# Attention with a top-1 expert layer on one core: a re-planned agenda of projections, with the bias moved to VectorE

## The chip, the core and the metric

One NeuronCore of a Trainium2 chip runs the whole kernel in one launch. The metric is the device time in microseconds. All data is fp32 unless a line says otherwise.

## The reference

`x` has the shape 4 x 2048 x 512. A layer norm without gain gives `xn`. Two branches read `xn`, and both are added to `x`:

```python
qkv = xn @ w_qkv                               # 16 heads of 32
q, k = spectral_filter(q, mask), spectral_filter(k, mask)
attn = softmax(q @ k.T / sqrt(32)) @ v
attention = attn @ w_out + b_out

probs = softmax(xn @ w_gate)                   # 8 experts, top 1, 100 slots each
expert = gate * (xn_of_slot @ w_expert + b_expert)   # first 100 tokens of each expert
out = x + attention + expert
```

The filter is a fixed 32 x 32 map on each head, so the kernel folds it once into the query and key columns of `w_qkv`.

## The kernel before

**Units of work.** Work is cut by batch (4) and by group of four heads (4 per batch): 16 groups, numbered `k`. For a group the kernel walks over four blocks of 512 queries, and in a block over 16 tiles of 128 keys. One key tile against 512 queries for four heads is called a *half* here (two of them make a `window` of the main loop). A block has 16 halves, a group 64, and the kernel 1024.

**What every half holds.** In order of emission, for the two pairs of heads: `max_matmuls` (two matmuls whose products only serve the row maxima, 40 items ahead of their use), `scores` (two matmuls into the four PSUM banks kept for scores), the exponential of those two heads on ScalarE, and `max_reduce` on VectorE. Then `products` (probabilities times values, of the half before) with `num += ...` on VectorE. Then whatever the agenda has for this half.

**Banks.** The other four PSUM banks go round in turn (`turns`, `bank()`): two for each `max_matmuls`, one for `products`, one for each further piece. A half with one piece takes six banks, one without takes five. `max_reduce` either reads both banks in one instruction, where they lie side by side (`joined`), or each by itself (`apart=True`), which lets the first go earlier.

**The agenda.** Before the main loop, `plan(k)` writes for every half which further pieces it emits. TensorE's pieces all cost about the same:

- `query_key` and `value`: 48 pieces a group, the projections of the next group (`projections(k + 1)` gives their order). `spread` places them by the costs already booked in each half, up to a half called `last`.
- `result`: 16 a group, a quarter of a block's output projection; `fold`: four a group, the sums of the probabilities. Both follow from the end of a block (`close_steps`): `fold` in its fifth half after, eight reciprocals (`invert`) in halves 6 to 13, results in halves 17 to 20.
- `turn`: 16 transposes of normalized rows in the last group of a batch.

Once per block the maxima are negated and transposed on TensorE (`max_close`, in the block's twelfth half), split into three bf16 parts on GpSimd (`max_split`) and sent by a small DMA (`negm<-row`); the next block begins with a matmul on them (`shift`).

**Around it.** GpSimd adds pairs of probability tiles (`even<-even`) after an accumulating DMA of its own queue (`even<-odd`) has added the odd tile to the even one. In the third group of a batch (k = 2, 6, 10) the next batch's rows are loaded on SP's queue, measured on VectorE (`measure`: `bn_stats`, `bn_aggr`), given the output bias on GpSimd (`bias`), and written to the output (`first_sums`); `scale` makes their factors on GpSimd. The first batch's rows get bias and first sums in group 0. Later every block's result is added to the output by an accumulating DMA from `y`.

All of these go through a helper that keeps each engine's program order, so nearly every instruction carries its line, 84. Tiles tell them apart.

Of the kernel before, what the change touches and what calls it, by code (L numbers as in the profile page):

```python
# [103 lines left out]
def attention_and_top1_experts(ctx: ExitStack, tc: tile.TileContext, a: dict, out: bass.AP):  # L104
# [90 lines left out]
    def filter_steps(c):  # L195

        held = {}

        def turned(s):
            if s == 0:  # L200
                held["wt"] = probs(c % 2 == 1)
            pt = bank()
            for r in range(NR):
                on.tensor.transpose(
                    pt[:, r * P : (r + 1) * P], raw[s, r // 2][:, r % 2, c * P : (c + 1) * P], ident
                )
            on.vector.tensor_copy(held["wt"][:, s, 0, :], pt)

        def filtered(s):
            pw = bank()  # L210
            wt = held["wt"][:, s]
            for r in range(NR):
                at = slice(r * P, (r + 1) * P)
                on.tensor.matmul(pw[:, at], lhsT=wt[:, 0, at], rhs=filt, start=True, stop=True)
            done = pw.rearrange("p (r n) -> p r n", r=NR)
            if c == 0:
                on.scalar.copy(wg[0][:, :, s, :], done)
# [12 lines left out]
    def token_stage(b):  # L230
# [19 lines left out]

        def bias(i):
            row = held[i // TQ][:, i % TQ, :]
            on.gpsimd.tensor_tensor(row, row, b_out, ALU.add)

        def first_sums(i):

            n, t = divmod(i, TQ)
            on.sync.dma_start(out=o[b, n, :, t : t + 1, :], in_=held[n][:, t : t + 1, :])

# [147 lines left out]
        route += [lambda i=i: enter(i) for i in range(NT)]  # L407
        return load, measure, scale, normalize, turn, route, bias, first_sums, load_tile

# [3 lines left out]

    def load_qkv_weights(k):
        wg[k] = weights.tile([P, NR, 3, P], F32, name="wg", bufs=1)
        on.sync.dma_start(out=wg[k], in_=wd[k % NG])

# [11 lines left out]
    def query_key(k, n, s, first, last):  # L429
# [3 lines left out]
        for r in range(NR):  # L433
            columns(pq, wg[k][:, r, s, :], xnT[:, r, cols], start=(r == 0), stop=(r == NR - 1))
        if s == 0:
# [16 lines left out]
    def value(k, n, first, last):  # L452
# [3 lines left out]
        for t in range(first, last):  # L456
            i = n * TQ + t
            for r in range(NR):
                columns(
                    pv[:, t * P : (t + 1) * P],  # L460
                    xnT[:, r, i * P : (i + 1) * P],
                    wg[k][:, r, 2, :],
                    start=(r == 0),
# [4 lines left out]

    def projections(k, tiles=1):

# [4 lines left out]
        else:  # L475
            late = [(value, n) for n in range(2, NQ)] + [(query_key, 1, 0)]
            order = [(query_key, 0, 0)] + [(value, n) for n in range(2)] + (late if k not in CROWDED else [])
            order += [(query_key, n, 1) for n in range(NQ)] + (late[::-1] if k in CROWDED else [])
            order += [(query_key, n, 0) for n in range(2, NQ)]
        return [  # L480
# [71 lines left out]
    def expert_steps():  # L552


        def begin():
            w_exp = chunk("w_exp")
            on.sync.dma_start(out=w_exp, in_=a["L0_ffn_w_expert"].rearrange("(r p) n -> p r n", p=P))
            b_exp = b_out
            on.sync.dma_start(out=b_exp, in_=a["L0_ffn_b_expert"].partition_broadcast(P))
# [129 lines left out]
    def close_steps(k, n):  # L689
# [49 lines left out]

    load, measure, scale, normalize, turn, first_route, first_bias, first_sums, load_tile = token_stage(0)  # L740

# [3 lines left out]
    load(3, probs(False).rearrange("p u h q -> p (u h) q"))  # L745
    wg[0] = weights.tile([P, NR, 3, P], F32, name="wg", bufs=1)
    nc.sync.dma_start(out=wg[0][:, :, 2, :], in_=w_qkv[:, :, 2 * DM : 2 * DM + P])
    for c in range(1, NG):
# [4 lines left out]
    for i in range(2 * NG + 1):  # L753
# [4 lines left out]
        if 2 * NG - TQ <= i < 2 * NG:  # L758
            measure(i - 2 * NG + TQ)
    nc.sync.dma_start(out=wd[0], in_=wg[0])  # L760
    first_projections = projections(0, TQ)
# [50 lines left out]
    for i, item in enumerate(stream[:MAX_AHEAD]):  # L812
# [5 lines left out]
        max_matmuls(item, half)  # L818
        max_reduce(item, half)
        if i in ahead:  # L820
# [81 lines left out]

    def keys_from(k):

        return (9 if k in CROWDED else 6) * TQ

    def plan(k):
# [3 lines left out]

        def after_keys_are_spent(steps, start):

            first = len(steps) - keys_from(k + 1)
            for i in range(NT):
                cost, _, step = steps[first + i]
                steps[first + i] = cost, start + SPENT + i // TQ * TQ, step

        if k == 0:
            for i in range(NT):  # L920
                half = 2 + i + 5 * (i // TQ)
                at(half, load_tile, i)
                at(half + 4, first_bias, i)
                at(half + 6, first_sums, i)
# [4 lines left out]
        steps = []  # L929
        if k == 0:  # L930
            done = spread([(1, 0, step) for step in first_projections], 15)
            at(done[-1] + 1, load_qkv_weights, 1)
            plan_route(20, lambda i: first_route[i]())
            ready = done[-1] + 3
        if c == NG - 2 and b + 1 < B:

            at(start + 20, begin_stage, b + 1)
            for i in range(NT):
                half = start + 20 + i + 5 * (i // TQ)
                at(half, in_stage, 8, i)  # L940
                at(half + 3, in_stage, 1, i)
                at(half + 4, in_stage, 6, i)
                at(half + 6, in_stage, 7, i)
            for n in range(NQ):
                at(start + 30 + (TQ + 5) * n, in_stage, 2, n * TQ, (n + 1) * TQ)
            for i in range(2 * TQ):
                at(start + GH - 6 + i, in_stage, 8, i)
        pieces = projections(k + 1)
        if c == NG - 1:

            late = {8: 9, 12: 14}
            order = [("turn", i) for i in range(8)] + pieces[:4] + [("turn", i) for i in range(8, 12)]
            order += pieces[4:8] + [("turn", i) for i in range(12, NT)] + pieces[8:]
            steps, first = [], start + 1
# [6 lines left out]
            steps[0] = (1, first, steps[0][2])  # L961
            after_keys_are_spent(steps, start)
            done = spread(steps, last)
# [3 lines left out]
            for i in range(2 * TQ, NT):  # L967
                at(turned[i // TQ * TQ - TQ - 1] + 1 + i % TQ, in_stage, 8, i)
            plan_route(turned[NT - 1] + 2, follow_route)
        else:  # L970
            steps = [(1, ready if k == 0 else start, step) for step in pieces]
            after_keys_are_spent(steps, start)
            done = spread(steps, last)
        assert done[-4] >= start + 3 * HB and done[-8] >= start + 2 * HB
        for i in range(NT):
            here = done[len(done) - keys_from(k + 1) + i] - start - i // TQ * TQ
            assert SPENT <= here < SPENT + 3 * TQ
# [35 lines left out]
    for k in range(B * NG):  # L1013
        for n in range(NQ):
            num = work.tile([P, QB], F32, tag="num", name="num")
            tiles = {}
            for w in range(NW):
# [9 lines left out]
                for j in (even, odd):  # L1027
# [5 lines left out]
                    for u in range(2):  # L1033
# [72 lines left out]
```

## Time and profile before

| what | value |
|---|---|
| time, median of 3 runs | 4277.05 us (4273.49 to 4280.85) |
| the profiled execution | 4282.12 us, of which the span 4280.0 us |
| TensorE busy | 4194.3 us (98%) |
| VectorE, ScalarE, GpSimd busy | 3411.0 (80%), 2525.3 (59%), 3037.6 (71%) |
| reductions of maxima, 128x512 apart / 128x1024 joined | 2576 of 683 ns / 760 of 1217 ns |
| GpSimd's bias, 128x512 | 64 of 1546 ns |
| ScalarE's copy of a result | 252 of 586 ns |
| VectorE's add of a PSUM bank, 128x512 (`num`) | 960 of 677 ns |

Matmuls overlap each other in the array, and a matmul that is slow to end counts as busy, so the 98% does not say that TensorE is at its peak. A half's length is better read in the timeline, from the first weight load of its `keys,q` matmuls to that of the next half.

### The profile page before, as it was taken

Reading aid. Unit: us, or ns where it says so; the run is one execution under the profiler, and the core shown is the slowest. Engines: PE = TensorE matmul, PEld = TensorE weight load, DVE = VectorE, ACT = ScalarE, POOL = GpSimd, SP = SyncE. Lnnn points to the kernel's source line nnn. Section 1 sums busy time; section 2 is a strip of 40 time slices with the busy share of each in tenths; the row PEclk is TensorE's granted clock in tenths of the full one; section 3 lists DMA queues with packets and bytes.
Section 4 is the critical chain, followed back from the end, with each engine's and each line's share of the span. In section 5 each row is a group of like instructions: output and inputs, shape, how many; then the busy total and the mean of one; then the engine's idle time right before and its main releaser. Section 6 shows DMA issues by size and latency. Waiting matters only on the chain.

```text
span 4280.0 us, 120579 instructions
## 1 busy us (share of the span) xinstructions
PE 4194.3 (98%) x52270; PEld 1854.3 (43%) x52270; DVE 3411.0 (80%) x5102; ACT 2525.3 (59%) x3475; POOL 3037.6 (71%) x2110
## 2 busy tenths in 40 slices
PE   8999999999999999999999999999999999999998
PEld 4444444434444444443444444443444444444432
DVE  6767888877788888887778888887778887788885
ACT  2556655666566556557556666555755565556665
POOL 1678777876776767777677766778668776676773
PEclk9999999999999999999999999999999999999999
DMA  4767778887687778888677787888877886778788
GB/s 109 179 149 152 153 160 173 191 201 151 137 159 153 156 152 165 182 195 186 132 158 151 158 159 146 170 188 194 170 140 152 175 164 131 148 162 161 154 168 167
DMA packets 163452, 690.16 MB, mean 161 GB/s; under 512 B 27414, under 2 KB 32696, under 8 KB 97640
## 3 DMA queue, kind: packets, MB, share of 16 engines
q0 software_dynamic: 110432, 605.83, 72.1%
q1 hardware_dynamic: 51312, 76.10, 5.7%
q8 instruction: 409, 6.70, 0.6%
q14 instruction: 123, 1.01, 0.1%
q10 hardware_dynamic: 1176, 0.52, 0.1%
HBM read 59.27 MB, written 88.96 MB: 35 GB/s over the span
## 4 chain that ended last, share of the span: by engine, by line
PE 89%; DVE 6%; DMA 2%; POOL 2%; issue 1%; ACT 0%; ACTq 0%; POOLq 0%; DVEq 0%
PE array L84 89%; DVE part L84 4%; DMA even<-odd 2%; POOL even L84 1%; DVE num L84 0%; DVE stats L84 0%; DMA negm<-row 0%; DVE factor L84 0%; POOL xs L84 0%; DMA odd<-in_L_attn_w_qkv_dram 0%; DVE mv L84 0%; POOL row L84 0%; POOL rstd L84 0%; DVE even L84 0%; POOL rest L84 0%
## 5 line engine op out<-in xcount | busy, mean ns | idle before, releaser
L84 DVE TENSOR_REDUCE part<-array 128x1 f32<-128x512 f32 (+1 forms) x3336 | 2497.1, 805 | 761.6 <-PE array L84 758.3
L84 POOL TENSOR_TENSOR even<-even 128x1024 f32<-128x1024 f32 x876 | 2121.5, 2524 | 425.9 <-DMA even<-odd 417.8
L84 PE MATMUL array<-keys,q 32*128 32x512 f32 x8192 | 2089.7, 615 | 10.9 <-DVE part L84 5.5
L84 PE MATMUL array<-q,steps_of_keys 32*128 32x512 f32 x8192 | 2022.7, 618 | 3.3 <-ACT odd L84 1.7
L84 ACT ACTIVATE even<-array 128x1024 f32<-128x1024 f32 x1024 | 993.5, 1021 | 491.3 <-PE array L84 455.6
L84 ACT ACTIVATE odd<-array 128x1024 f32<-128x1024 f32 x1024 | 993.3, 1021 | 458.8 <-PE array L84 378.5
L84 PEld LDWEIGHTS array<-keys,q 32*128 32x128 f32 x8192 | 784.3, 185 | 591.3 <-DVE part L84 365.3
L84 PEld LDWEIGHTS array<-q,steps_of_keys 32*128 32x128 f32 x8192 | 707.2, 184 | 267.3 <-issue 233.1
L84 POOL DMA_DIRECT2D even<-odd x510 | 463.4, 909 | 402.2 <-ACT odd L84 321.4
L84 DVE TENSOR_TENSOR num<-num,array 128x512 f32<-128x512 f32 x960 | 650.3, 677 | 26.3 <-PE array L84 17.2
L84 PE MATMUL array<-odd,v 128*32 128x512 f32 x4096 | 549.4, 608 | 2.4 <-DVE part L84 2.4
L84 PE MATMUL array<-even,v 128*32 128x512 f32 x4096 | 547.4, 606 | 2.9 <-DVE part L84 2.9
L84 PEld LDWEIGHTS array<-xnT,wg 128*32 128x32 f32 x15808 | 439.0, 110 | 256.2 <-DVE part L84 176.2
L84 PE MATMUL array<-xnT,wg 128*32 128x128 f32 (+1 forms) x15808 | 522.0, 277 | 11.4 <-DVE part L84 10.6
L84 PEld LDWEIGHTS array<-wg,xnT 128*32 128x32 f32 x8192 | 227.9, 110 | 129.2 <-DVE part L84 94.4
L84 DVE RECIPROCAL factor<-den 128x64 f32<-128x64 f32 x504 | 274.3, 545 | 0.0
L84 PE MATMUL array<-wo,ot 128*32 128x512 f32 x2048 | 267.8, 596 | 4.0 <-POOL ot L84 4.0
L84 PE MATMUL array<-wg,xnT 128*32 128x128 f32 x8192 | 263.5, 273 | 4.4 <-DVE part L84 4.4
L84 PEld LDWEIGHTS array<-odd,v 128*32 128x32 f32 x4096 | 81.0, 108 | 394.1 <-DVE part L84 384.9
L84 PEld LDWEIGHTS array<-even,v 128*32 128x32 f32 x4096 | 80.8, 108 | 393.8 <-DVE part L84 382.7
L84 POOL DMA_DIRECT2D out_dram<-y x63 | 83.7, 1329 | 212.4 <-ACT y L84 190.9
L84 ACT COPY y<-array 128x512 f32<-128x512 f32 x252 | 147.5, 586 | 139.8 <-PE array L84 139.4
(129 smaller groups left out, 1490.5 us busy)
## 6 DMA issues: line engine op xcount, KB each, us to landing
even<-odd POOLq DMA_DIRECT2D x510, 1024.0 KB, 8.2
out_dram<-y POOLq DMA_DIRECT2D x63, 1024.0 KB, 10.1
xs<-in_L_attn_x_dram SPq DMA_DIRECT2D x112, 256.0 KB
out_dram<-xs SPq DMA_DIRECT2D x64, 256.0 KB
wg<-wd SPq DMA_DIRECT2D x15, 768.0 KB
wo<-in_L_attn_w_out_dram SPq DMA_DIRECT2D x16, 256.0 KB
negm<-row SPq DMA_DIRECT2D x192, 4.0 KB
xs<-in_L_attn_x_dram SPq DMA_DIRECT2D x2, 1024.0 KB
```

What stands on the lines that cost most here:

```text
L84: done = act(*args, **kwargs)
```

## The change

- `load_qkv_weights`: the next group's weights lie in three tiles (query, key, value), each loaded by itself when its own last piece is done.
- `projections`: most groups begin with all value pieces, then half of the queries, the keys, and the rest of the queries. `last` is the group's last half and no longer the fourth from its end; the extra cost booked in the half of `max_close` is 0.25 and no longer 0.5; a `turn` is booked at 0.5 and no longer at 1.
- `max_close` comes behind the half's agenda, not ahead of it.
- `bias` on GpSimd is gone: where k is a multiple of 4 (the first head group of a batch) `result` adds `b_out` on VectorE and the ScalarE copy is not made. `first_sums` is one DMA of 1 MB from the input to the output for each 512 rows, not four of 256 KB from SBUF. In group 0 the rows are not loaded again for it.
- In groups 2, 6 and 10 `measure` moves from halves 23 to 53 to halves 30 to 37 and 46 to 53, where no reciprocals are planned.
- `max_reduce` reads apart in every half for which nothing was booked; ahead of the main loop it reads joined wherever it can.
- The experts' bias has a tile of its own.

```diff
 def load_qkv_weights(k, s):
-    wg[k] = weights.tile([P, NR, 3, P], F32, name="wg", bufs=1)
-    on.sync.dma_start(out=wg[k], in_=wd[k % NG])
+    wg[k, s] = weights.tile([P, NR, P], F32, name=f"w{s}", bufs=1)
+    on.sync.dma_start(out=wg[k, s], in_=wd[k % NG][:, :, s, :])
...
-def bias(i):
-    row = held[i // TQ][:, i % TQ, :]
-    on.gpsimd.tensor_tensor(row, row, b_out, ALU.add)
-def first_sums(i):
-    n, t = divmod(i, TQ)
-    on.sync.dma_start(out=o[b, n, :, t : t + 1, :], in_=held[n][:, t : t + 1, :])
+def first_sums(n):
+    on.sync.dma_start(out=o[b, n], in_=x[b, n])
...
 def projections(k, tiles=1, kinds=None):
     ...
-    late = [(value, n) for n in range(2, NQ)] + [(query_key, 1, 0)]
-    order = [(query_key, 0, 0)] + [(value, n) for n in range(2)] + (late if k not in CROWDED else [])
-    order += [(query_key, n, 1) for n in range(NQ)] + (late[::-1] if k in CROWDED else [])
-    order += [(query_key, n, 0) for n in range(2, NQ)]
+    first = 2 if k in CROWDED else 3 if k % NG == 0 else 4
+    queries, vals = ([(f, n, *s) for n in range(NQ)] for f, *s in ((query_key, 0), (value,)))
+    news = [(query_key, n, 1) for n in range(NQ)]
+    if first == 4:
+        order = vals + queries[:2] + news + queries[2:]
+    else:
+        order = vals[:first] + queries[:1] + news[:3]
+        order += vals[first : first + 1] + news[3:] + vals[first + 1 :] + queries[1:]
...
-def max_reduce(item, half):
+def max_reduce(item, half, apart=True):
-    whole = joined(*half) if u == 0 else joined(*half, apart=True)
-    for heads, products_of in whole:
+    for heads, products_of in joined(*half, apart):
...
 def result(t):
-    on.scalar.copy(held["y"][:, t, :], project(k, held["ot"], t))
+    if k % NG == 0:
+        on.vector.tensor_tensor(held["y"][:, t, :], project(k, held["ot"], t), b_out, ALU.add)
+    else:
+        on.scalar.copy(held["y"][:, t, :], project(k, held["ot"], t))
...
-        max_reduce(item, half)          # ahead of the main loop
+        max_reduce(item, half, False)
...
 def plan(k):
     if k == 0:
-        for i in range(NT):
-            half = 2 + i + 5 * (i // TQ)
-            at(half, load_tile, i); at(half + 4, first_bias, i); at(half + 6, first_sums, i)
+        for n in range(NQ):
+            at(2 + (TQ + 5) * n, first_sums, n)
-    last = start + GH - 4
+    last = start + GH - 1
     if c == NG - 2 and b + 1 < B:
         for i in range(NT):
-            half = start + 20 + i + 5 * (i // TQ)
-            at(half, in_stage, 8, i); at(half + 3, in_stage, 1, i)    # load, measure
-            at(half + 4, in_stage, 6, i); at(half + 6, in_stage, 7, i) # bias, first_sums
-        for n in range(NQ):
-            at(start + 30 + (TQ + 5) * n, in_stage, 2, n * TQ, (n + 1) * TQ)   # scale
+            half = start + 2 * HB - 2 + i + 8 * (i // (NT // 2))
+            at(half - 4, in_stage, 7, i); at(half, in_stage, 1, i)    # load, measure
+            if i % TQ == TQ - 1:
+                n = i // TQ
+                at(half + 1, in_stage, 2, n * TQ, (n + 1) * TQ)       # scale
+                at(half - 2, in_stage, 6, n)                          # first_sums
...
-                steps.append((1, start + late[i] if i in late else 0, lambda i=i: in_stage(4, i)))
+                steps.append((0.5, start + late[i] if i in late else 0, lambda i=i: in_stage(4, i)))
...
-        at(done[-1] + 1, load_qkv_weights, k + 2)
+        for s in range(3):
+            at(places[s][-1] + 1, load_qkv_weights, k + 2, s)
...
-    costs[block * HB - 4] += 0.5
+    costs[block * HB - 4] += 0.25
...                                      # main loop
-            max_reduce(mate, mh)
+            max_reduce(mate, mh, u == 0 or not costs[2 * window + (j == odd)])
...
         left = k, n, j, tiles[j], num
+        for step in agenda[2 * window + (j == odd)]:
+            step()
         if j == even and window in full:
             splits[window + 1] = full.pop(window)
             max_close(*splits[window + 1])
-        for step in agenda[2 * window + (j == odd)]:
-            step()
```

The built program of the changed kernel shows where `spread` puts the pieces. Over the 1004 halves that still have `max_matmuls` (without the 56 in each program that hold transposes, routing or expert work), so many halves have this many pieces (`query_key`, `value`, `result`, `fold`):

| pieces in a half | 0 | 1 | 2 | 3 | 4 |
|---|---|---|---|---|---|
| before | 124 | 639 | 173 | 10 | 2 |
| after | 77 | 744 | 123 | 0 | 4 |

Of the 62 halves with `max_close`, 49 have pieces or transposes beside it, before and after. The halves with four pieces are all at key pieces: one `qqqq` in half 32 of group 0 and one in its half 44 before; half 32 of groups 0, 3, 7 and 11 after.

More of the change, by code (lines that the diff above doesn't have):

```diff
@@ L216, in filtered @@
             if c == 0:
-                on.scalar.copy(wg[0][:, :, s, :], done)
+                on.scalar.copy(wg[0, s], done)
             else:
@@ L407, in token_stage, with load_qkv_weights @@
         route += [lambda i=i: enter(i) for i in range(NT)]
-        return load, measure, scale, normalize, turn, route, bias, first_sums, load_tile
+        return load, measure, scale, normalize, turn, route, first_sums, load_tile
     qs, vs = {}, {}
     wo = {}
-    def load_qkv_weights(k):
-        wg[k] = weights.tile([P, NR, 3, P], F32, name="wg", bufs=1)
-        on.sync.dma_start(out=wg[k], in_=wd[k % NG])
+    def load_qkv_weights(k, s):
+        wg[k, s] = weights.tile([P, NR, P], F32, name=f"w{s}", bufs=1)
+        on.sync.dma_start(out=wg[k, s], in_=wd[k % NG][:, :, s, :])
     def load_out_weights(k):
@@ L433, in query_key @@
         for r in range(NR):
-            columns(pq, wg[k][:, r, s, :], xnT[:, r, cols], start=(r == 0), stop=(r == NR - 1))
+            columns(pq, wg[k, s][:, r, :], xnT[:, r, cols], start=(r == 0), stop=(r == NR - 1))
         if s == 0:
@@ L461, in value @@
                     xnT[:, r, i * P : (i + 1) * P],
-                    wg[k][:, r, 2, :],
+                    wg[k, 2][:, r, :],
                     start=(r == 0),
@@ L467, in value, with projections @@
         on.scalar.copy(vs[k][:, n * TQ + first : n * TQ + last, :], done)
-    def projections(k, tiles=1):
+    def projections(k, tiles=1, kinds=None):
+        kinds = [] if kinds is None else kinds
         if k == 0:
@@ L475, in projections @@
         else:
-            late = [(value, n) for n in range(2, NQ)] + [(query_key, 1, 0)]
-            order = [(query_key, 0, 0)] + [(value, n) for n in range(2)] + (late if k not in CROWDED else [])
-            order += [(query_key, n, 1) for n in range(NQ)] + (late[::-1] if k in CROWDED else [])
-            order += [(query_key, n, 0) for n in range(2, NQ)]
+            first = 2 if k in CROWDED else 3 if k % NG == 0 else 4
[6 more added lines that the diff above has]
+                order += vals[first : first + 1] + news[3:] + vals[first + 1 :] + queries[1:]
+        kinds.extend((2 if f is value else at[1]) for f, *at in order for t in range(0, TQ, tiles))
         return [
@@ L557, in begin @@
             on.sync.dma_start(out=w_exp, in_=a["L0_ffn_w_expert"].rearrange("(r p) n -> p r n", p=P))
-            b_exp = b_out
+            b_exp = work.tile([P, DM], F32, tag="b_exp", name="b_exp", bufs=1)
             on.sync.dma_start(out=b_exp, in_=a["L0_ffn_b_expert"].partition_broadcast(P))
@@ L737, in close_last @@
                 on.sync.dma_start(out=o[b, n, :, t - 1 : t + 1, :], in_=y[:, t - 1 : t + 1, :])
-    load, measure, scale, normalize, turn, first_route, first_bias, first_sums, load_tile = token_stage(0)
+    load, measure, scale, normalize, turn, first_route, first_sums, _ = token_stage(0)
     load(0)
@@ L745, in attention_and_top1_experts @@
     load(3, probs(False).rearrange("p u h q -> p (u h) q"))
-    wg[0] = weights.tile([P, NR, 3, P], F32, name="wg", bufs=1)
-    nc.sync.dma_start(out=wg[0][:, :, 2, :], in_=w_qkv[:, :, 2 * DM : 2 * DM + P])
+    for s in range(3):
+        wg[0, s] = weights.tile([P, NR, P], F32, name=f"w{s}", bufs=1)
+    nc.sync.dma_start(out=wg[0, 2], in_=w_qkv[:, :, 2 * DM : 2 * DM + P])
     for c in range(1, NG):
@@ L759, in attention_and_top1_experts @@
             measure(i - 2 * NG + TQ)
-    nc.sync.dma_start(out=wd[0], in_=wg[0])
+    for s in range(3):
+        nc.sync.dma_start(out=wd[0][:, :, s, :], in_=wg[0, s])
     first_projections = projections(0, TQ)
@@ L901, in place_experts @@
                 free += 2
-    def keys_from(k):
-        return (9 if k in CROWDED else 6) * TQ
     def plan(k):
@@ L910, in plan, with after_keys_are_spent @@
         start = k * GH
-        def after_keys_are_spent(steps, start):
-            first = len(steps) - keys_from(k + 1)
-            for i in range(NT):
-                cost, _, step = steps[first + i]
-                steps[first + i] = cost, start + SPENT + i // TQ * TQ, step
-        if k == 0:
-            for i in range(NT):
-                half = 2 + i + 5 * (i // TQ)
-                at(half, load_tile, i)
-                at(half + 4, first_bias, i)
-                at(half + 6, first_sums, i)
+        def after_keys_are_spent():
+            for i, place in enumerate([j for j, s in enumerate(kinds) if s == 1]):
+                cost, _, step = steps[place]
+                steps[place] = cost, start + SPENT + i // TQ * TQ, step
+        if k == 0:
+            for n in range(NQ):
+                at(2 + (TQ + 5) * n, first_sums, n)
         if k + 1 == B * NG:
@@ L927, in plan @@
         at(start + GH // 2, load_out_weights, k + 1)
-        last = start + GH - 4
-        steps = []
+        last = start + GH - 1
+        steps, kinds = [], []
         if k == 0:
             done = spread([(1, 0, step) for step in first_projections], 15)
-            at(done[-1] + 1, load_qkv_weights, 1)
+            for s in range(3):
+                at(done[-1] + 1, load_qkv_weights, 1, s)
             plan_route(20, lambda i: first_route[i]())
@@ L938, in plan @@
             for i in range(NT):
-                half = start + 20 + i + 5 * (i // TQ)
[L940 to L943, printed above, removed]
-            for n in range(NQ):
-                at(start + 30 + (TQ + 5) * n, in_stage, 2, n * TQ, (n + 1) * TQ)
+                half = start + 2 * HB - 2 + i + 8 * (i // (NT // 2))
+                at(half - 4, in_stage, 7, i)
+                at(half, in_stage, 1, i)
+                if i % TQ == TQ - 1:
+                    n = i // TQ
+                    at(half + 1, in_stage, 2, n * TQ, (n + 1) * TQ)
+                    at(half - 2, in_stage, 6, n)
             for i in range(2 * TQ):
-                at(start + GH - 6 + i, in_stage, 8, i)
-        pieces = projections(k + 1)
+                at(start + GH - 6 + i, in_stage, 7, i)
+        pieces = projections(k + 1, kinds=kinds)
         if c == NG - 1:
@@ L953, in plan @@
             order += pieces[4:8] + [("turn", i) for i in range(12, NT)] + pieces[8:]
+            kinds = [None] * 8 + kinds[:4] + [None] * 4 + kinds[4:8] + [None] * 4 + kinds[8:]
             steps, first = [], start + 1
@@ L957, in plan @@
                     i = step[1]
-                    steps.append((1, start + late[i] if i in late else 0, lambda i=i: in_stage(4, i)))
+                    steps.append((0.5, start + late[i] if i in late else 0, lambda i=i: in_stage(4, i)))
                 else:
                     steps.append((1, 0, step))
-            steps[0] = (1, first, steps[0][2])
-            after_keys_are_spent(steps, start)
+            steps[0] = (0.5, first, steps[0][2])
+            after_keys_are_spent()
             done = spread(steps, last)
@@ L967, in plan @@
             for i in range(2 * TQ, NT):
-                at(turned[i // TQ * TQ - TQ - 1] + 1 + i % TQ, in_stage, 8, i)
+                at(turned[i // TQ * TQ - TQ - 1] + 1 + i % TQ, in_stage, 7, i)
             plan_route(turned[NT - 1] + 2, follow_route)
@@ L971, in plan @@
             steps = [(1, ready if k == 0 else start, step) for step in pieces]
-            after_keys_are_spent(steps, start)
+            after_keys_are_spent()
             done = spread(steps, last)
         assert done[-4] >= start + 3 * HB and done[-8] >= start + 2 * HB
-        for i in range(NT):
-            here = done[len(done) - keys_from(k + 1) + i] - start - i // TQ * TQ
-            assert SPENT <= here < SPENT + 3 * TQ
+        places = [[h for h, s in zip(done, kinds) if s == kind] for kind in range(3)]
+        for i, h in enumerate(places[1]):
+            assert SPENT <= h - start - i // TQ * TQ < SPENT + 3 * TQ
+        assert places[0][3] < start + GH - MAX_AHEAD // 2 and places[0][7] < start + GH + HB - MAX_AHEAD // 2
         for n in range(NQ):
@@ L980, in plan @@
         if k + 2 < B * NG:
-            at(done[-1] + 1, load_qkv_weights, k + 2)
+            for s in range(3):
+                at(places[s][-1] + 1, load_qkv_weights, k + 2, s)
     SPENT = GH - HB - MAX_AHEAD // 2 + TQ
```

## The prediction

> **What bounds the kernel now.** I read the page's busy times first.
>
> ```profile
> PE 4194.3 (98%) x52270; PEld 1854.3 (43%) x52270; DVE 3411.0 (80%) x5102; ACT 2525.3 (59%) x3475; POOL 3037.6 (71%) x2110
> ```
>
> TensorE looks full, so I looked in the timeline at what a half costs, and whether its length follows TensorE's work. First the weight loads that open four halves of group 5; the first three hold one piece each (`value`), the one from 1516.15 to 1520.82 holds two.
>
> ```profile
> 1508.55 0.19 PEld L84 LDWEIGHTS array<-keys,q 32*128 32x128 f32 x2 [0.20 <-DVE part L84]
> 1512.35 0.19 PEld L84 LDWEIGHTS array<-keys,q 32*128 32x128 f32 x2 [0.20 <-DVE part L84]
> 1516.15 0.19 PEld L84 LDWEIGHTS array<-keys,q 32*128 32x128 f32 x2 [0.20 <-DVE part L84]
> 1520.82 0.19 PEld L84 LDWEIGHTS array<-keys,q 32*128 32x128 f32 x2 [0.20 <-issue]
> ```
>
> A half with one piece lasts 3.80 us and ends when VectorE frees banks (`<-DVE part`); one with two lasts 4.67 and ends when TensorE has issued its work. I cut all 1024 halves this way: one piece 3.80 (median of 595), two 4.67 (of 172), each further one 0.87 more, none 3.49 (of 112; singly 2.9 to 3.9). The first piece of a half costs 0.31 us, the second 0.87: below one piece the bank cycle through VectorE sets the length, above it TensorE. VectorE's side of such a half:
>
> ```profile
> 1508.25 0.68 DVE L84 TENSOR_TENSOR num<-num,array 128x512 f32<-128x512 f32 x1
> 1508.85 0.55 DVE L84 RECIPROCAL factor<-den 128x64 f32<-128x64 f32 x1
> 1509.71 2.42 DVE L84 TENSOR_REDUCE part<-array 128x1 f32<-128x512 f32 x3 [0.32 <-PE array L84]
> ```
>
> The three reductions (two apart, one joined) end at 1512.13, the next half's matmuls start 0.2 later, and their products can be reduced 1.2 us after that. In this gap of 1.4 us VectorE has room for the add and 0.7 us more.
>
> Second, a half with `max_close`, from its opening load to the next one's:
>
> ```profile
> 1465.01 0.19 PEld L84 LDWEIGHTS array<-keys,q 32*128 32x128 f32 x2 [0.20 <-DVE part L84]
> 1467.51 0.09 PEld L84 LDWEIGHTS array<-square,neg 128*16 128x16 f32 x1 [0.42 <-DVE part L84]
> 1468.64 0.81 PEld L84 LDWEIGHTS array<-wg,xnT 128*32 128x32 f32 x32 [0.72 <-DVE part L84]
> 1469.65 0.19 PEld L84 LDWEIGHTS array<-keys,q 32*128 32x128 f32 x2 [0.20 <-issue]
> ```
>
> 4.64 us: the close takes the second bank that comes free and the projection behind it waits 0.72 for the third, which the joined reduction frees last; so the 0.85 us of projection lie bare. Of the 49 such halves with pieces, 30 are 0.84 to 0.9 longer than without a close, 12 are 0.48 to 0.49, seven other; 39 us in all.
>
> Third, the stretches of group 5, group 6, and a piece right behind group 6:
>
> ```profile
> core 0: us, PE busy (x) PEld busy (x) DVE busy (x) ACT busy (x) POOL busy (x), PEclk, DMA share, GB/s
> 1417.74:1669.93 252.19, 250.86 (x3259) 110.43 (x3259) 207.40 (x306) 151.97 (x208) 179.09 (x117) 1.00 0.79 156
> 1669.93:1932.54 262.61, 253.52 (x3258) 110.89 (x3258) 219.46 (x338) 151.87 (x208) 201.47 (x147) 1.00 0.85 183
> 1932.20:1938.30 6.10, 5.78 (x28) 1.64 (x28) 2.52 (x3) 2.05 (x2) 6.10 (x4) 0.50 0.92 236
> ```
>
> Group 6 does the same TensorE work and takes 10.4 us more; GpSimd has 22 us more, DMA 0.06 more. Why, the timeline at its end shows:
>
> ```profile
> 1886.96 1.26 POOL L84 TENSOR_TENSOR xs<-xs,b_out 128x512 f32<-128x512 f32 x1
> 1929.21 0.42 POOL L84 TENSOR_TENSOR rest<-rest,row 16x128 f32<-16x128 f32 x1
> 1932.52 0.61 PE L84 MATMUL array<-negm,ones_b 3*128 3x512 bf16 x4 [5.60 <-DMA negm<-row]
> ```
>
> GpSimd, late with its adds, reaches `max_split` at 1929.21, 12 us after the close; the next block's `shift` waits 5.6 us for it, and TensorE's granted clock is 0.50 for the next 6 us.
>
> **The change part by part**, against the profiled execution's 4282.1 us.
>
> *Spreading.* With the counts of the built programs: before 124 x 3.49 + 639 x 3.80 + 173 x 4.67 + 10 x 5.54 + 2 x 6.42 = 3737; after 77 x 3.49 + 744 x 3.80 + 123 x 4.67 + 4 x 6.42 = 3696. But 17 pieces have gone into halves with transposes or routing (1023 pieces before, 1006 after): 17 x 0.87 = 15. **-26 us.** Ends -20 and -32: an empty half at 3.35 to 3.63.
>
> *Close behind the agenda.* The projection takes the second bank at its usual time and covers the wait for the third; the close (0.38 of matmuls) follows just when the joined reduction ends. What is late next: the next half's second `keys,q` bank is now that of `products`, freed by `num` 0.7 us after the reduction, and the scores queue behind it on TensorE; of this 0.5 us about 0.3 is slack (`products` waits 0.76 for VectorE anyway). I take 0.2 us for each of 49, ends 0 and 0.49 (the cheap kind of today): 39 - 10, **-29 us**, ends -39 and -15.
>
> *Bias off GpSimd, statistics away from reciprocals.* Groups 2, 6 and 10 last 260.5, 262.6 and 261.4 against 252.2, and the half behind each is 2 us long: 34 us. Some 0.3 us each are halves in which `bn_stats` (0.66) and `bn_aggr` (0.18) meet a reciprocal; they move to halves with 0.77 free. The rest is GpSimd's lag, and 16 x 1.55 = 25 us of GpSimd work a group go, more than the 22 it has too much. The bytes on SP's queue stay, now as four copies of 1 MB from DRAM to DRAM, an operation the trace does not have. Nearest rows: 256 KB of `out_dram<-xs`, and `even<-odd` of 1 MB, 8.2 us to landing. I leave 6 of the 34 us, **-28**; ends -34 and 0 (above it: a rival).
>
> *The bias on VectorE.* 64 adds from PSUM, 677 ns by the row of `num`, in halves without reciprocals:
>
> ```profile
> 1501.11 0.58 ACT L84 COPY y<-array 128x512 f32<-128x512 f32 x1 [0.66 <-PE array L84]
> 1502.13 2.42 DVE L84 TENSOR_REDUCE part<-array 128x1 f32<-128x512 f32 x3 [0.77 <-PE array L84]
> ```
>
> The add fits into the 0.77. But its bank comes free 0.35 later than by ScalarE's copy, and the second `keys,q` and the scores behind it wait for that; TensorE then reaches `products` some 0.08 late. 64 x 0.08 = **+5 us**, ends 0 and 43 (0.68 each, if the cover is gone). ScalarE's 37 us less are off the path.
>
> *Halves with four pieces.* Half 32 of group 0 took 8.99 against 6.5, and the two behind it 3.7 too much:
>
> ```profile
> 239.08 1.13 PE L84 MATMUL array<-keys,q 32*128 32x512 f32 x4
> 241.66 1.38 PE L84 MATMUL array<-q,steps_of_keys 32*128 32x512 f32 x8 [1.46 <-issue]
> ```
>
> The scores at 241.66 wait for no semaphore: behind 128 short matmuls TensorE had no instructions, and from 242.5 the granted clock was 0.50 for 6.8 us. 6.2 us in all. The other such half, 44 of group 0, lost nothing. Four halves after, at one in two: 4 x 3.1 - 6.2 = **+6**, ends -6 and +19. [...]
>
> *The rest.* Transposes at half cost pack three with two normalizations into one half of groups 3, 7 and 11 (three x 0.59 + two x 0.81 + two exponentials x 1.02 = 5.4 us of ScalarE in a half of 4.9): **+4**, ends 0 and 8. Apart reductions in 77 empty halves: four cost 2.48 against 2.42, the third bank comes 0.5 us earlier: **-6**, ends 0 and -15. Joined ahead of the loop: 20 x 0.06, **-1**, ends -3 and +2. Weights in three loads have 16 halves until their use, and the b_exp tile only takes space: nothing; a late load would show as 1 to 5 us a group.
>
> Sum: -26 - 29 - 28 + 5 + 6 + 4 - 6 - 1 = -75, so 4207 by the profiled execution. That one is 5 us above the median: **4202 us**.
>
> **The rivals.**
> 1. *The lag stays.* The DMA share was 0.89 in the last block of group 6, and the adds on GpSimd waited for `even<-odd`; if SP's bytes are the cause and not the bias, the 28 us stay: 4230. Against: GpSimd was itself busy for 54 of those 69 us.
> 2. *The close only changes places.* If the next half pays for the bank of `num` in full and scores run late into the following one, the 29 us stay: 4231. Against: the 0.76 of slack.
> 3. *Slower: the 1 MB copies.* If each of the 16 delays the accumulating DMAs by so much that a `shift` comes late, each costs what the end of group 2 cost, 6.2 us in its last half and 2.0 behind (half clock): 131 on top of rival 1, 4361. From six such stalls on, the change loses. Against: 256 KB stores of the same bytes, four at a time, are there today and most blocks pass.
> 4. *No effect.* If the 98% were real, pieces could not be had cheaper anywhere: 4277. Against: 3.49, 3.80 and 4.67.
>
> **The numbers.** The forecast 0.62, rivals 0.15, 0.12, 0.05 and 0.06 in this order. What this measurement can tell from no change is about 0.2% (8.6 us). Faster takes the first three cases but 0.01: 0.88; same 0.04 and slower 0.08, from rival 4 on both sides of nothing, rival 3, and the bias at its far end. The range: all favourable ends give 4155, but not all at once; 4170 below; 4248 above takes in rivals 1 and 2 with another 17 us of bias or fetch.
>
> **What would show it.** Halves with one piece still at 3.80; halves with a close and a piece at 4.0 and not 4.64, the half behind under 4.0; group 6 within 3 us of group 5, and no 0.50 clock at the ends of groups 2, 6 and 10; bias halves within 0.1 of 3.78. It is wrong if PEclk falls at blocks that have a copy from DRAM to DRAM, if `shift` waits longer for `negm<-row`, or if half 32 of groups 3, 7 and 11 lasts 9 us each.

## The result, and the profile after

The changed kernel takes 4234.16 us in the median of four runs (4231.54 to 4236.65), beside 4277.45 us for the kernel before: a ratio of 0.9899 (0.9882 to 0.9916), 43 us less. The direction was forecast and the size was not: 75 us less were (4202 us). The profiled execution took 4234.09 us, its span 4232.3; against the 4280.0 of before the span is 47.7 us shorter.

The page's busy times of the changed kernel:

```profile
PE 4175.4 (99%) x52270; PEld 1866.6 (44%) x52270; DVE 3453.9 (82%) x5199; ACT 2489.9 (59%) x3411; POOL 2958.5 (70%) x2046
```

GpSimd has the 64 instructions of `bias` less (2110 to 2046) and 79 us less to do; ScalarE has 64 copies less (3475 to 3411), and VectorE makes them. TensorE's share has even risen to 99%, which tells as little as the 98% did: the page books 8192 `keys,q` matmuls of 616 ns as 2085.4 us busy, where one after another they would be 5046.

I cut the trace into halves (the 1004 that hold `max_matmuls`), here at the first weight load of the scores, which in a plain half comes 0.01 us behind that of `keys,q`, and sorted them by what they hold. A *stall* is what a half takes over the mean of its class before, where that is more than 0.6 us; such a half counts in its class with that mean alone. *Special* halves hold transposes, routing or the expert layer.

| class | before: halves, mean us | after: halves, mean us | change of the sum, us |
|---|---|---|---|
| no piece | 112, 3.448 | 65, 3.301 | |
| one piece | 595, 3.806 | 698, 3.817 | |
| two | 172, 4.678 | 123, 4.694 | |
| three; four | 10, 5.57; 1, 6.52 | none; 4, 6.52 | these four rows: -35.2 |
| special | 56, 4.98 | 56, 5.29 | +17.4 |
| close and pieces | 46, 4.65 | 46, 4.25 | -18.5 |
| close alone | 12, 3.68 | 12, 3.73 | +0.6 |
| stalls | 36.5 us | 28.1 us | -8.4 |

That is -44.1 us; the other 3.6 of the span lie ahead of these halves and behind them. Three places carry the difference from the forecast, and each is seen in the trace. First, a half with `max_close`, in the timeline. It opens at 1451.24; the next one's `keys,q` follow at 1455.23, its scores (`q,steps_of_keys`) at 1455.53, and at 1459.32 the half after that:

```profile
1451.24 0.19 PEld L84 LDWEIGHTS array<-keys,q 32*128 32x128 f32 x2 [0.20 <-DVE part L84]
1453.74 0.13 PEld L84 LDWEIGHTS array<-w,xnT 128*32 128x32 f32 x4 [0.41 <-DVE part L84]
1454.80 0.68 DVE L84 TENSOR_TENSOR num<-num,array 128x512 f32<-128x512 f32 x1
1454.82 0.20 PEld L84 LDWEIGHTS array<-square,neg 128*16 128x16 f32 x2
1455.23 0.47 PEld L84 LDWEIGHTS array<-keys,q 32*128 32x128 f32 x3 [0.21 <-issue]
1455.53 0.19 PEld L84 LDWEIGHTS array<-q,steps_of_keys 32*128 32x128 f32 x2
1459.32 0.19 PEld L84 LDWEIGHTS array<-keys,q 32*128 32x128 f32 x2 [0.20 <-issue]
```

The piece (`w,xnT`) now waits 0.41 us for its bank, as in a plain half, and no longer 0.72, and the close (`square,neg`) follows it. But the close's own matmuls hold the next `keys,q` up until 1455.23, and the scores behind the second of them come only when `num` has freed its bank (1454.80 + 0.68 = 1455.48). Cut at the scores the half lasts 4.28 us (median of such halves 4.22, before 4.65) and the next one 3.80; cut at `keys,q`, as ahead of the prediction, it is 3.99 and 4.09, the same sum (medians 4.00 for such halves and 4.02 for the halves behind them, where a plain half takes 3.80).

Second, the end of group 6. The timeline, and what GpSimd waited for in the last block (us in total, times, longest):

```profile
1905.21 0.42 POOL L84 TENSOR_TENSOR rest<-rest,row 16x128 f32<-16x128 f32 x1
1908.57 0.61 PE L84 MATMUL array<-negm,ones_b 3*128 3x512 bf16 x4 [4.81 <-DMA negm<-row]
```

```profile
POOL even L84 <- DMA even<-odd: 17.8, 5, 5.2
```

`shift` still waits 4.8 us (5.6 before) for `max_split`, which GpSimd reaches late, with less work of its own: it waits 17.8 us in this block for its accumulating transfers, 13.9 before. The granted clock still falls to 0.50 at the ends of groups 2, 6 and 10, from 880.96, 1908.37 and 2932.37 us on. Groups 2, 6 and 10 take 253.1, 254.4 and 254.1 us, group 5 takes 249.8.

Third, group 0, with half 32 of four pieces. TensorE's timeline:

```profile
239.76 0.59 PE L84 MATMUL array<-keys,q 32*128 32x512 f32 x2
242.42 1.08 PE L84 MATMUL array<-q,steps_of_keys 32*128 32x512 f32 x4 [2.06 <-issue]
```

The stop for which the profile names no wait (`<-issue`, 1.46 us before, 2.06 here) has come back, one half later: half 33 takes 10.3 us, 6.5 too many. The same halves of groups 3, 7 and 11, which also hold four pieces now, take 6.52 us and nothing stalls behind them.

A half with a bias, in the timeline of group 4, goes as forecast:

```profile
1291.36 0.69 DVE L84 TENSOR_TENSOR y<-array,b_out 128x512 f32<-128x512 f32 x1
1291.98 0.30 PEld L84 LDWEIGHTS array<-keys,q 32*128 32x128 f32 x2 [0.24 <-issue]
1292.16 1.29 DVE L84 TENSOR_REDUCE part<-array 128x1 f32<-128x512 f32 x2
```

The add (`b_out`) lies between `num`, which VectorE begins at 1290.77, and the next reductions; its bank comes free at 1292.05, 0.07 us after the next half's opening load.

### The profile page after: what moved, and what is told of

Its sections match the earlier page's. It is cut to its first block, busy times and chain, and to the rows that moved or that the text cites. A ratio compares the mean times of both kernels' runs of the same rounds, so it can differ in the third digit from the quotient of the medians.

```text
span 4232.3 us, 120483 instructions
## 1 busy us (share of the span) xinstructions
PE 4175.4 (99%) x52270; PEld 1866.6 (44%) x52270; DVE 3453.9 (82%) x5199; ACT 2489.9 (59%) x3411; POOL 2958.5 (70%) x2046
## 4 chain that ended last, share of the span: by engine, by line
PE 88%; DMA 5%; POOL 3%; DVE 2%; issue 1%; ACT 0%; POOLq 0%; ACTq 0%; DVEq 0%
PE array L84 88%; DMA even<-odd 4%; POOL even L84 2%; DVE part L84 1%; POOL rstd L84 0%; DVE stats L84 0%; DVE num L84 0%; POOL ot L84 0%; DMA odd<-in_L_attn_w_qkv_dram 0%; DVE factor L84 0%; POOL steps_of_keys L84 0%; DMA negm<-row 0%; POOL rest L84 0%; POOL row L84 0%; ACT odd L84 0%
## 5 line engine op out<-in xcount | busy, mean ns | idle before, releaser
L84 PE MATMUL array<-keys,q 32*128 32x512 f32 x8192 | 2085.4, 616 | 8.5 <-DVE part L84 4.9
L84 PEld LDWEIGHTS array<-xnT,w 128*32 128x32 f32 x15808 | 444.6, 110 | 259.5 <-DVE part L84 165.0
L84 PE MATMUL array<-xnT,w 128*32 128x128 f32 (+1 forms) x15808 | 522.2, 277 | 0.9 <-ACT xnT L84 0.7
L84 PEld LDWEIGHTS array<-w,xnT 128*32 128x32 f32 x8192 | 230.7, 110 | 146.4 <-DVE part L84 103.5
L84 PE MATMUL array<-w,xnT 128*32 128x128 f32 x8192 | 269.3, 273 | 1.3 <-DVE num L84 1.2
L84 ACT COPY y<-array 128x512 f32<-128x512 f32 x188 | 110.0, 585 | 104.2 <-PE array L84 104.1
```

The costliest lines, as they stand in the source:

```text
L84: done = act(*args, **kwargs)
```

## The experiments

The kernel before took 4279 to 4281 us beside them; ratios are to it. Microseconds saved or lost against the changed kernel are to its 4234.16 us, which come from an earlier session in which the kernel before took 4277.45; so differences of under some 5 us from the changed kernel can't be told from none by the times alone.

**The close alone.** In the kernel before, only the order of the two blocks is changed:

```diff
+                    for step in agenda[2 * window + (j == odd)]:
+                        step()
                     if j == even and window in full:
                         splits[window + 1] = full.pop(window)
                         max_close(*splits[window + 1])
-                    for step in agenda[2 * window + (j == odd)]:
-                        step()
```

> The kernel before with one part of the change alone: max_close behind the half's agenda. Theory A (as in the prediction: the projection covers the wait, the next half absorbs most of what the bank of num costs): a half with close and pieces lasts 4.0 us, 29 us off, 4248. Theory B (read from the changed kernel: the close's own matmuls delay the next half's first head by 0.2 us, and its second head and the scores behind it wait 0.3 for num, and none of it is absorbed): such halves last 4.22 to 4.29, 39 us of excess become about 21, 18 us off, 4259. Theory C (the close was covered by the other parts, not by this one): within 5 us of 4277.

4263.5 us, 0.9964 (0.9952 to 0.9977): 15.7 us less, and close halves of 4.22 us. The move brings about half of what I took, whatever the rest of the change does.

**What an earlier end of the close would bring.** A projection fills only one quarter of its bank (128 of 512 columns), so behind such a piece the close can write into a quarter that is free. In one kernel the close stays behind the agenda and goes into that bank:

```diff
-        pn = bank()[0 : HG * TQ, 0:P]
+        if spare[1] is None:
+            pn = bank()[0 : HG * TQ, 0:P]
+        else:
+            pn = array[0 : HG * TQ, spare[0], spare[1] * P : (spare[1] + 1) * P]
```

> The changed kernel, with the close writing its 16 x 128 products into a free quarter of the bank of the projection just ahead of it, where there is one, so that it takes no bank of its own and the next half's banks are those of a half without a close. Theory B (0.2 of the 0.42 us are the close's matmuls, the rest is the wait for num): halves with close and piece 4.22 to about 3.95 to 4.05, 8 to 11 us off, 4224. If the 0.42 is all matmul time: within 3 us of 4234. If the shared bank comes free later, because ScalarE has three copies to make of it, and the next half's matmuls wait for that: slower than the changed kernel.

4242.1 us, 0.9916 (0.9903 to 0.993): slower than the changed kernel by 8. Its close halves take 4.58 us; in its timeline the close now waits for ScalarE's copy out of the same bank:

```profile
1518.83 0.11 PEld L84 LDWEIGHTS array<-square,neg 128*16 128x16 f32 x2 [0.65 <-ACT q L84]
```

One bank saved, and 0.65 us lost: I had not counted the copy that lies between. In the other kernel the close's matmuls are emitted ahead of that copy, right behind the projection's:

```diff
             columns(pq, wg[k, s][:, r, :], xnT[:, r, cols], start=(r == 0), stop=(r == NR - 1))
+        if last == first + 1:
+            ride(last % TQ)      # the close's matmuls, into that quarter of this bank
```

> The changed kernel with the close's two matmuls emitted between a projection's matmuls and its copy, into a free quarter of the same bank: no bank of its own, and nothing for TensorE to wait for (in the run before with one shared bank it waited 0.65 for ScalarE's copy). Theory B (0.2 of the 0.42 us are the close's matmuls, the rest the wait for num's bank): halves with close and piece 4.22 to 4.0, 46 x 0.22 = 10 us off, 4224. If the rest was not that wait: 4234.

4223.6 us, 0.987 (0.9855 to 0.9885), 10.6 us less than the changed kernel. Its timeline shows one such half, 1508.95 to 1512.96:

```profile
1508.95 0.19 PEld L84 LDWEIGHTS array<-keys,q 32*128 32x128 f32 x2 [0.20 <-DVE part L84]
1512.53 0.21 PEld L84 LDWEIGHTS array<-square,neg 128*16 128x16 f32 x2
1512.94 0.19 PEld L84 LDWEIGHTS array<-keys,q 32*128 32x128 f32 x2 [0.21 <-issue]
1512.96 0.19 PEld L84 LDWEIGHTS array<-q,steps_of_keys 32*128 32x128 f32 x2
```

4.00 us in the median, the length that I had forecast for the change. The next half's loads of `keys,q` and of the scores are 0.02 us apart and no longer 0.30: the 0.22 us between 4.22 and 4.00 was the wait for the bank of `num`, and what is left over a plain half, 0.2, goes to the close's own two matmuls.

**The transfers of the next batch's rows.** The 1 MB copies of groups 2, 6 and 10 go into groups 1, 5 and 9:

```diff
+        if c == NG - 3 and b + 1 < B:
+            for n in range(NQ):
+                at(start + 6 + n * HB, copy_rows, b + 1, n)
...
-                    at(half - 2, in_stage, 6, n)
```

> The changed kernel, with the four copies from input to output of the next batch moved from groups 2, 6 and 10 (halves 31 to 51) to groups 1, 5 and 9 (halves 6, 22, 38, 54); the bytes are the same. Theory A (what is left of the stalls at the ends of groups 2, 6 and 10, 18 us in three, comes from the bytes on the DMA engines there, 0.90 to 0.93 busy, that hold back even<-odd and so GpSimd): the DMA share there falls to about 0.87, the last halves of these groups lose their 4 us each and the first of the next its 1 to 2, 12 to 18 us off, 4216 to 4222. Theory B (GpSimd's own instructions or the loads of rows alone do it): 0 to 5 us off, 4229 to 4234, the 0.50 clock at the three ends stays.

4213.6 us, 0.9849 (0.9836 to 0.9863), 20.6 us less than the changed kernel. Groups 2, 6 and 10 take 249.2 us each, as the others, and the 0.50 clock at their ends is gone. So bytes of SP's queue do matter. Were they what held the kernel before up, too? There I took out GpSimd's 64 adds of the bias alone and left the loads and stores (the output lacks the bias, here and in one kernel below):

```diff
-                at(half + 4, first_bias, i)
...
-                at(half + 4, in_stage, 6, i)
```

> The kernel before without the 64 bias instructions on GpSimd (the bias is left out; loads, stores and statistics stay as they are). It tests the step of the prediction that gave the lag of groups 2, 6 and 10 to GpSimd's own work. Theory GpSimd (as predicted): 25 us of GpSimd work a group less than the 22 too many, the waits at the three ends and the 0.50 clock go, 20 to 28 us off, 4250 to 4258. Theory DMA (from the run with the copies moved): the stores and loads are still there, most of the waits stay, 0 to 10 us off, 4268 to 4277.

4252.3 us, 0.9936 (0.9922 to 0.9949), 26.5 us less than before: the waits at all three ends are gone, and the three groups take 254.0, 254.4 and 254.8 us. The old lag was GpSimd's work, as I had said; the lag of the changed kernel is another one. Two more kernels ask what made it. One puts loads, statistics, factors and copies of the stage back to their old halves (20 to 57), with the copies still of 1 MB from DRAM to DRAM:

```diff
-                half = start + 2 * HB - 2 + i + 8 * (i // (NT // 2))
-                at(half - 4, in_stage, 7, i); at(half, in_stage, 1, i)
+                half = start + 20 + i + 5 * (i // TQ)
+                at(half, in_stage, 7, i); at(half + 3, in_stage, 1, i)
...
-                    at(half - 2, in_stage, 6, n)
+                    at(half + 6, in_stage, 6, n)
```

> The changed kernel with the loads, statistics, factors and copies of groups 2, 6 and 10 at the halves of the kernel before (20 to 56), the copies still 1 MB from DRAM to DRAM. Theory times (the later and denser loads make the DMA engines late at the group's end): the 18 us of waits at the three ends go for the most part, and the halves in which statistics meet reciprocals cost 2 to 3 us a group: 4222 to 4228. Theory copies (the 1 MB copies do it wherever they lie in these groups): the waits stay, 4234 to 4242.

The other keeps the new times and stores the rows from SBUF in 256 KB, as before:

```diff
+                at(half + 1, in_stage, 8, i)      # 256 KB, out of held[n]
...
-                    at(half - 2, in_stage, 6, n)
```

> The changed kernel with the first sums of groups 2, 6 and 10 as 16 stores of 256 KB from SBUF, each one half behind its measurement, and everything else at the changed kernel's times; group 0 keeps its copies. Theory copies: a copy from DRAM to DRAM holds the DMA engines longer than a store of the same bytes, so the waits at the three ends go for the most part: 4218 to 4224. Theory times: the waits stay, 4231 to 4237.

The old times: 4227.9 us, 0.9874 (0.9859 to 0.9889), 6.3 us less than the changed kernel; the three waits are gone, and the halves outside the stalls cost some 10 us more, 7 of them in groups 2, 6 and 10, where statistics meet reciprocals again. The stores: 4234.6 us, 0.9884 (0.9869 to 0.99), the waits as they were (4.9 us of `shift` at the end of group 6). The times made the lag and not the form of the transfer; which of the four things that moved together matters most was not run. In the last block of group 6, `even<-odd` in the changed kernel (above) cost 17.8 us of waiting; with the copies moved away, with the old times, and with the stores, in this order:

```profile
POOL even L84 <- DMA even<-odd: 14.1, 5, 3.5
```

```profile
POOL even L84 <- DMA even<-odd: 12.8, 3, 5.3
```

```profile
POOL even L84 <- DMA even<-odd: 16.8, 5, 5.2
```

And the windows of the last two blocks of group 6, of the changed kernel and then of the one with the old times:

```profile
core 0: us, PE busy (x) PEld busy (x) DVE busy (x) ACT busy (x) POOL busy (x), PEclk, DMA share, GB/s
1778.51:1841.78 63.27, 62.83 (x854) 28.18 (x852) 57.78 (x95) 38.25 (x53) 43.77 (x36) 1.00 0.92 211
1841.78:1908.59 66.81, 61.69 (x790) 27.21 (x788) 57.55 (x93) 37.92 (x52) 47.84 (x38) 1.00 0.91 205
```

```profile
1778.00:1842.46 64.46, 62.87 (x850) 27.98 (x848) 57.26 (x95) 38.25 (x53) 47.22 (x37) 1.00 0.90 201
1842.46:1904.06 61.60, 61.60 (x790) 27.14 (x788) 54.25 (x86) 37.95 (x52) 45.52 (x37) 1.00 0.94 210
```

GpSimd has 91.6 us of work in these two blocks of the changed kernel and waits 18.1 and 17.8 us for `even<-odd`: 127.5 of 130.1 us. With the old times it is 92.7 and 13.0 + 12.8: 118.5 of 126.1. So where GpSimd had 2.6 us of slack in two blocks `shift` waited 4.8 us, and where it had 7.6 it did not. The DMA share alone doesn't tell the two apart (0.94 with the old times, and no stall). Why the accumulating transfers land later at the new times stays open. SP's queue stands on `negm<-row` from 1829.37 to 1839.41 and then issues four loads and two copies of 1 MB in 5.3 us; but with the old times it issues the same six in 4.3 us from 1835.30 on, so that burst alone does not tell the two apart.

**The burst of four pieces.** In group 0, the pieces of the first keys, which fell into half 32 all four, are kept one to a half:

```diff
-                steps[place] = cost, start + SPENT + i // TQ * TQ, step
+                steps[place] = cost, start + SPENT + i // TQ * TQ + (i % TQ if k == 0 else 0), step
```

> The changed kernel, with the first key pieces of group 0 due one half after the other, so that its half 32 holds one key piece and not four; groups 3, 7 and 11 keep their four. Theory A (128 short matmuls in a row run TensorE out of instructions there): the 6.5 us of half 33 and the 0.50 clock behind it go, 6 to 8 us off, 4227. Theory B (the instructions come late at this place whatever the half holds, for example because of what the DMA engines do then): the stall moves by a half or two and stays, 4234.

4225.8 us, 0.9877 (0.9862 to 0.9892), 8.4 us less. The stop at 240 and the half clock at 242 are gone, and group 0 takes 272.7 us instead of 279.4.

**The bias on VectorE.** The result is copied by ScalarE in every group (`if False` for `if k % NG == 0`), so the output bias is left out:

> The changed kernel without the output bias: result is ScalarE's copy in all groups, b_out is left out. It prices the 64 adds on VectorE. As in the prediction (the add fits into the gap, its bank comes free 0.35 later): 3 to 5 us off, 4230. If the adds cost their 0.68 each: 43 us off, 4191. If they cost nothing: within 2 us of 4234.

4227.65 us, 0.9881 (0.9866 to 0.9896): 6.5 us less, hardly more than can be told. By it the 64 adds cost 0.1 us each; I took 0.08.

**Apart reductions.** Empty halves are read joined again (`max_reduce(mate, mh, u == 0)`):

> The changed kernel with one part undone: in halves with nothing booked the second pair of banks is read joined again where it can be. It prices the apart reductions, which the prediction put at 6 us. Theory small: 4234 to 4240. Theory large (read from the run with the old order: its empty halves lasted 3.28 us without stalls, those of the kernel before 3.45, and nothing else differs in them): 65 halves x 0.17 and those with only a shift or a close besides, 11 to 15 us more than the changed kernel, 4245 to 4249.

4238.8 us, 0.9899 (0.9884 to 0.9914): 4.6 us more by the times and nothing by the ratio, so no clear difference. Empty halves take 3.44 us joined and 3.30 apart, 9 us over the 65 of them. The large loss did not come; the small one that I forecast fits, but is not shown apart from none.

**The order of projections.** The old order, and `last` three halves earlier again:

```diff
-    last = start + GH - 1
+    last = start + GH - 4
...
+            late = [(value, n) for n in range(2, NQ)] + [(query_key, 1, 0)]
...
```

> The changed kernel with the order of projections of the kernel before and its last half for them (the fourth from the end of the group); all else as changed. It prices the spreading. 114 halves without a piece and 145 with two, against 77 and 123. By the lengths of halves (3.30 without stalls, 3.80, 4.67): 15 to 20 us more than the changed kernel, 4250 to 4254. If the spreading did nothing: 4234.

4235.3 us, 0.9902 (0.9887 to 0.9917): no change that can be measured, where a loss was expected. The table of classes, made for this kernel, says why. Its halves do cost more, 3.5 us in the classes and the special ones and 7.1 in those with a close; but its stalls come to 17.1 us instead of 28.1. The waits in the last halves of groups 2, 6 and 10 are 2.0, 2.7 and 1.6 us instead of 3.9, 4.4 and 4.5. So what the spreading saves in the halves is spent at these ends, where the next block waits for GpSimd: with the old order GpSimd is less late there, and waits 16.4 and 15.6 us for `even<-odd` in the last two blocks of group 6 and not 18.1 and 17.8. Why those transfers land sooner is not shown, and whether the spreading pays once the ends no longer wait was not run.

**The three mended.** Copies early, burst split and the close ahead of the copy, in one kernel:

> The changed kernel with the three repairs together: copies of rows in groups 1, 5 and 9, group 0's first key pieces one by one, the close riding in a projection's bank. Each alone took 20.6, 8.4 and 10.6 us off. If they are independent: 39 us, 4195. If the copies' gain and the others meet in the same waits: 4200 to 4210.

4202.6 us (4201.4 to 4205.9), 0.9815 (0.9801 to 0.9828): 31.6 us less than the changed kernel, 79 less than before, and the best version here. The three alone sum to 39.6; the stalls are down to 5 us and close halves at 4.03. Of the missing 8, some 5 lie in group 0: with the copies moved it already took 276.8 us and not 279.4, a part of the same stop that the split burst removes, and with all three it takes 274.0, not the 272.7 of the split alone. The rest lies in no wait that I could name.

## Why the prediction was right in sign and too large in size

- **What bounds the kernel: right.** A piece costs less in a half that has none (0.36 us by the means before, 0.52 after) than in one that has one (0.87 and 0.88); halves with one and two pieces stayed within 0.02 us of before, and the empty ones became shorter, as forecast. Rival 4 (no effect) falls.
- **Spreading: right in the halves, not in the time.** With the means of before, the new counts give -35.4 for the four classes (measured -35.2) and special halves +17.4: -18, where the sum had -26 and +4 for the transposes. But the kernel with the old order is as fast within what can be told: the term left out that what the halves save turns into waiting wherever a late GpSimd ends the block.
- **Bias on VectorE, apart reductions: not contradicted,** 6.5 for 5, and 4.6 by the times (nothing by the ratio) for 6. Halves with a bias take 3.85 us without group 0's stall, the plain ones 3.81.
- **Close behind the agenda: -18.5 instead of -29.** The step that failed is "of this 0.5 us about 0.3 is slack". The 0.5 was about right (4.28 against 3.80 above, 0.42 in the median) and none of it is slack: 0.2 us are the close's own matmuls and 0.22 the wait for `num`'s bank, and the kernel that saves the bank gains just that. Cut as in the prediction, the half with the close lasts the 4.0 us forecast, and the half behind it pays the 0.22. Scores that come late make the exponentials late and with them the cycle of the half; that `products` wait 0.76 us for VectorE further down takes none of it back (argued from the order, only the loss itself is shown). Rival 2's wait is there, but takes back 0.22 of the 0.65 us saved and not all of it.
- **Bias off GpSimd: cause right, remainder wrong.** Over group 5, the three groups and the half behind each took 34 us too much before and 18 after, so 16 us went and not 28; I had left 6. The failed step is the sentence that SP's bytes stay: they stay in number and not in time. Loads and copies now come together around the starts of the third and fourth block, and the mechanism of rival 1 took the place of the one removed, in part. Rival 3 did not come: three block ends wait, as before, and the form of the copies makes no difference.
- **Four pieces: +1 instead of +6.** It was one half in four that stalled and not one in two, but its stall grew from 6.2 to 7.2 us. That TensorE had no instructions there was my reading of a row that names no wait (1.46 us before, 2.06 after). Nor does a run show the "fetch" in the range; what they show is this stop, in one group of four, and that it is gone with the burst split. Why the same 128 short matmuls stop TensorE in one group only stays open. In group 0 a packet of the DMA queue that the page lists as `q8 instruction` comes 7.4 us after half 32 begins, in the others 6.8 to 8.7 after, which does not tell them apart.

Of the signs named beforehand, one-piece halves at 3.80, close halves at 4.0 (cut at `keys,q`), bias halves near the plain ones and half 32 of groups 3, 7 and 11 at 6.5 came true; the half behind a close under 4.0 (4.02), group 6 within 3 us of group 5 (4.6), and no half clock at the three ends did not. One sign of being wrong came too: the clock falls at the end of blocks that hold a copy from DRAM to DRAM, though at the same three ends as before, and with stores in place of the copies just so. One sum was wrong: all favourable ends give 4148 (4282.1 - 129 - 5), not 4155; nothing else hangs on it.

## What to carry to other kernels

When work is moved in time, write down where its transfers go as well as its instructions, and add up busy time and waits of the engine that receives them: here they filled 127.5 of 130.1 us, and the next block waited. Ask whether slack lies ahead of the point that ends the iteration; the wait of 0.76 us further down in the same half bought nothing here. And as long as a late engine ends the block, time saved elsewhere may only turn into waiting for it, so mend the late engine first.

## What the runs showed of the hardware

- In the changed kernel a burst of 128 short matmuls was followed by a stop of TensorE of 2.06 us, for which the profile names no wait, in one group of four, and that cost 7 us: the granted clock was 0.50 for 6.83 us from 242.66 us on. In the kernel before the stop was 1.46 us, and the clock was 0.50 for 6.83 us from 242.47 on.
- At the ends of groups 2, 6 and 10 of the changed kernel, where `shift` waits 4.28, 4.81 and 4.92 us, the granted clock was 0.50 for 6.83, 3.41 and 6.83 us. Why it was so for half as long at the second of them is not shown.
- Sixteen 256 KB stores from SBUF and four 1 MB copies from DRAM to DRAM a group disturb the accumulating transfers alike at the same times (16.8 and 17.8 us of waits in the last block of group 6).
- Two 128x512 reductions in place of one joined cost 0.06 us more on VectorE (2.48 for 2.42 us a half) and shorten an empty half by 0.14 us (3.44 to 3.30); that the bank which comes free earlier does it is argued.
